# Last-hop finishes spread out and normed in place, remainder products and gates listed later, in a four-layer graph network on one core

## The chip, the cores and the metric

One NeuronCore of a Trainium2 chip runs the whole network as one launch. The metric is device time in microseconds, the median of several executions.

## The reference, cut to what matters

2708 nodes with 512 features, a dense fp32 matrix `adj` (2708 x 2708), four layers, each a residual with a layer norm:

```python
x = _layernorm(x + L0(x, adj))                # adj @ x with masked norms
x = _layernorm(x + L1(x, adj, adj, ...))      # gated: sigmoid(attn_a * x_a + attn_b * x_b)
x = _layernorm(x + L2(x, adj, weight))        # x@w0 + adj@x@w1 + adj^2@x@w2 + adj^3@x@w3: three hops
x = _layernorm(x + L3(x, adj, deg, W, b))     # relu((a_norm @ x + x) @ W + b)
```

## The kernel before

Each sweep over `adj` is cut into block products in a Strassen-like scheme, so that VectorE forms sums and differences of blocks (`z`, `s`, `t`) and TensorE multiplies them into four PSUM homes called u, c, d and a. The two sweep ranges of a hop have seven products each. Work is *listed*: `at(position, function)` puts a step at a position, one product being two units long, and a scheduler then orders each engine's instructions from that list. What happens is decided by the order that comes out, not by the listed number itself.

When an output block is complete, its *finish* runs in the product that follows: six tiles are transposed back (`ps_n`), added to their residual `ld`, normed, stored to `X3`, transposed again (`ps_t`) and stored to `X3T`. The last hop has four groups of such finishes.

```python
def nat(nm):                                    # six buffers of [128, 512] in all
    return pool.tile([P, D], F32, name=nm, tag="nat", bufs=6)

def fetch2(src, h, r0, w):                      # a tile of w rows, cut where it crosses a 128-row block
    o = nat("ld")
    for t, a, b, m in split(h, r0, w):          # m = 128, 82, 46, 36, 92, 83, 119, 74 or 9 rows
        nc.sync.dma_start(out=o[b : b + m, :], in_=src[t][a : a + m, :])
    return o

def done5(p0, dp, g, i0, n, h, cc, tiles):      # the finishes of the last hop
    for i, (s, lo, w) in enumerate(tiles):
        ...
        def a(...): got["x"] = fetch2(X2, h, r0, w)
        def b(...):
            ps = untranspose2(cc, s, lo, w)     # ps_n
            y = got["x"]
            nc.vector.tensor_tensor(y[:w], ps[:w], y[:w], ALU.add)
            o = nat("o")
            layernorm([(o, 0, D)], y, w, True)  # VectorE, GpSimd (power), VectorE, ScalarE
            store2(X3, o, h, r0, w)
            got["o"] = o
        def c(...): store_T(X3T[...], transposed([(got["o"], 0, D)], w)[:, :, :w])   # ps_t
        p = p0 + dp * i                         # dp = 0.15, for the last group 0.12
        at(p - 0.3, a); at(p, b); at(p + 0.5, c)
```

The loads of z for the next products stand in the same SyncE queue as these fetches:

```python
nc.sync.dma_start(out=t[:w, :n], in_=src)       # w = 128, or 74 for the remainder rows; a ring of 38 tiles
```

## Time and profile before

| | |
|---|---|
| time before | 3113.19 us (median of 3, 3111.91 to 3114.22) |
| span of the profiled execution | 3116.2 us |
| TensorE idle | 150 us of the span; the list of its waits adds up to 129 us, 22 of them in the counting at the start |
| waits in the finishes of the last hop | 46.0 us (ps_t, ps_n L1051) |
| waits of the second layer's gates (pz) | 16.9 us |
| waits of the remainder product (accu L987) | 15.2 us |

The number that matters is the idle time of TensorE with its aftermath (the slow clock after a wait: 0.80 to 0.87 granted in the four finish products of the last hop, 1.00 in a product without a wait), since it is busy for 95% of the span and every other engine has room (VectorE, the next, is busy for 70%). The prediction shows the lines.

### The profile page before, as it was taken

Reading aid. Unit: us, or ns where it says so; the run is one execution under the profiler, and the core shown is the slowest. Engines: PE = TensorE matmul, PEld = TensorE weight load, DVE = VectorE, ACT = ScalarE, POOL = GpSimd, SP = SyncE. Lnnn points to the kernel's source line nnn. Section 1 sums busy time; section 2 is a strip of 40 time slices with the busy share of each in tenths; the row PEclk is TensorE's granted clock in tenths of the full one; section 3 lists DMA queues with packets and bytes.
Section 4 is the critical chain, followed back from the end, with each engine's and each line's share of the span. In section 5 each row is a group of like instructions: output and inputs, shape, how many; then the busy total and the mean of one; then the engine's idle time right before and its main releaser. Section 6 shows DMA issues by size and latency. Waiting matters only on the chain.

```text
span 3116.2 us, 37246 instructions
## 1 busy us (share of the span) xinstructions
PE 2965.9 (95%) x10982; PEld 1943.1 (62%) x10982; DVE 2194.5 (70%) x5396; ACT 601.7 (19%) x1149; POOL 550.9 (18%) x985
## 2 busy tenths in 40 slices
PE   7999989999999999999999999999998898899995
PEld 5755655557665666766666666666665565565553
DVE  5889787565557676774776768767776576778684
ACT  4554100000154554531000000000001100101000
POOL 1423233232310101213101030011201202300000
PEclk9999999999999999999999999999999899999998
DMA  7665456556554334645766585566755556755551
GB/s 220 209 191 171 140 175 188 136 141 140 168 104 127 108 111 119 195 140 185 221 182 197 178 250 166 177 208 184 229 167 179 175 175 191 213 168 187 155 167 62
DMA packets 363251, 529.75 MB, mean 170 GB/s; under 512 B 49730, under 2 KB 309274, under 8 KB 363048
## 3 DMA queue, kind: packets, MB, share of 16 engines
q1 hardware_dynamic: 305020, 380.81, 42.9%
q0 software_dynamic: 48736, 135.73, 13.2%
q10 hardware_dynamic: 9292, 10.84, 1.1%
q8 instruction: 87, 1.43, 0.2%
q14 instruction: 116, 0.95, 0.1%
HBM read 436.81 MB, written 90.37 MB: 169 GB/s over the span
## 4 chain that ended last, share of the span: by engine, by line
PE 80%; DMA 9%; DVE 6%; issue 3%; POOL 1%; ACT 1%; SPq 0%; ACTq 0%; POOLq 0%; DVEq 0%
PE accd L982 11%; PE accc L982 10%; PE accu L982 10%; PE ps_d L470 8%; PE accu L342 8%; PE accd L342 7%; PE accc L342 7%; PE acca L982 5%; PE acca L342 4%; DMA ld<-X 2%; DMA z<-As 2%; DMA a<-in_adjT 1%; PE accu L987 1%; PE accd L987 1%; PE acca L987 1%
## 5 line engine op out<-in xcount | busy, mean ns | idle before, releaser
L942 DVE TENSOR_TENSOR z<-z 128x339 f32<-128x339 f32 (+1 forms) x966 | 463.6, 508 | 56.3 <-DMA z<-As 28.7
L982 PE MATMUL accc<-z,t 128*128 128x338 f32 (+1 forms) x644 | 216.3, 455 | 0.0
L424 POOL TENSOR_TENSOR rstd<-rstd,neg_half 128x1 f32<-128x1 f32 (+3 forms) x92 | 57.9, 630 | 848.9 <-DVE rstd L423 846.0
L982 PE MATMUL accu<-z,t 128*128 128x338 f32 (+1 forms) x644 | 199.6, 456 | 0.2 <-DVE z L942 0.2
L982 PE MATMUL accd<-z,t 128*128 128x338 f32 (+1 forms) x644 | 196.9, 448 | 0.1
L982 PE MATMUL accc<-s,t 128*128 128x338 f32 (+1 forms) x644 | 195.8, 448 | 0.8 <-DVE s L942 0.8
L306 DVE TENSOR_TENSOR a<-a,a 128x384 f32<-128x384 f32 (+4 forms) x363 | 178.6, 515 | 18.5 <-PE accu L342 15.9
L1008 ACT COPY q<-accu 128x338 f32<-128x338 f32 (+1 forms) x84 | 34.3, 443 | 783.4 <-PE accu L982 783.4
L942 DVE TENSOR_TENSOR s<-z 128x338 f32<-128x338 f32 (+1 forms) x322 | 153.6, 507 | 30.5 <-PE accc L982 15.5
L982 PEld LDWEIGHTS accc<-z,t 128*128 128x128 f32 x644 | 123.6, 193 | 62.9 <-issue 4.0
L1014 DVE TENSOR_TENSOR q<-q,accd 128x338 f32<-128x338 f32 (+1 forms) x112 | 56.4, 504 | 150.3 <-PE accd L982 149.9
L982 PEld LDWEIGHTS accu<-z,t 128*128 128x128 f32 x644 | 123.2, 194 | 60.2 <-issue 3.8
L982 PEld LDWEIGHTS accc<-s,t 128*128 128x128 f32 x644 | 120.4, 190 | 58.2 <-DVE s L942 1.6
L982 PEld LDWEIGHTS accd<-z,t 128*128 128x128 f32 x644 | 119.8, 190 | 56.9 <-issue 1.2
L732 DVE SCALAR_TENSOR_TENSOR deg<-a,deg 128x384 f32<-128x384 f32 (+5 forms) x168 | 82.4, 506 | 80.5 <-DMA a<-in_adjT 80.0
L797 ACT ACTIVATE e<-row,neg_s 128x384 f32<-128x384 f32 (+5 forms) x176 | 100.5, 571 | 82.1 <-DVE e L799 24.0
L799 DVE TENSOR_TENSOR e<-e,f 128x384 f32<-128x384 f32 (+5 forms) x176 | 87.6, 506 | 27.6 <-ACT f L798 26.3
L798 ACT ACTIVATE f<-row,neg_s 128x384 f32<-128x384 f32 (+5 forms) x176 | 99.9, 568 | 12.7 <-PE accc L342 6.2
L309 POOL DMA_DIRECT2D As<-a x132 | 70.9, 540 | 130.5 <-DVE a L306 83.5
L1064 ACT COPY y<-ps_n 128x512 f32<-128x512 f32 (+2 forms) x48 | 28.1, 585 | 326.4 <-issue 176.3
L553 DVE SCALAR_TENSOR_TENSOR s<-a,row 128x384 f32<-128x384 f32 (+5 forms) x168 | 83.4, 509 | 9.8 <-ACT row L541 8.2
L800 DVE SCALAR_TENSOR_TENSOR a<-a,e 128x384 f32<-128x384 f32 (+5 forms) x176 | 87.9, 507 | 2.3
(632 smaller groups left out, 6060.6 us busy)
## 6 DMA issues: line engine op xcount, KB each, us to landing
z<-As SPq DMA_DIRECT2D x320, 169.5 KB
z<-As SPq DMA_DIRECT2D x320, 169.0 KB
a<-in_adjT SPq DMA_DIRECT2D x240, 192.0 KB
z<-in_adjT SPq DMA_DIRECT2D x240, 169.5 KB
z<-in_adjT SPq DMA_DIRECT2D x240, 169.0 KB
a<-in_adjT SPq DMA_DIRECT2D x120, 165.0 KB
cl<-in_adjT POOLq DMA_DIRECT2D x80, 192.0 KB, 4.5
a<-in_adjT SPq DMA_DIRECT2D x113, 128.0 KB
```

The source lines that it names most:

```text
L306: nc.vector.tensor_tensor(A[r, dst, k][:w, :n], A[r, a, k][:w, :n], A[r, b, k][:w, :n], op)
L342: nc.tensor.matmul(B[home, c][:, :n], X[STAT[p], k][:w, c * P : (c + 1) * P], A[r, MOV[p], k][:w, :n], start=bool(start and k == k0), stop ...
L470: nc.tensor.matmul(o, lhs(c), r, start=c == 0 and n == 0, stop=c == DC - 1, skip_group_check=True)
L553: nc.vector.scalar_tensor_tensor(t[:w, :n], a[:w, :n], 0.0, row[R0, h][:w, :n], ALU.is_gt, ALU.mult)
L732: nc.vector.scalar_tensor_tensor(d[:w, :n], a[:w, :n], 0.0, d[:w, :n], ALU.not_equal, ALU.add)
L797: nc.scalar.activation(e[:w, :n], row[R0, h][0][:w, :n], AF.Exp, bias=neg_s[:w, t : t + 1])
L798: nc.scalar.activation(f[:w, :n], row[R0, h][1][:w, :n], AF.Exp, bias=neg_s01[:w, t : t + 1])
L799: nc.vector.tensor_tensor(e[:w, :n], e[:w, :n], f[:w, :n], ALU.min)
L800: nc.vector.scalar_tensor_tensor(a[:w, :n], a[:w, :n], 0.0, e[:w, :n], ALU.not_equal, ALU.mult)
L942: nc.vector.tensor_tensor(d[:, :n], Z[x + (k,)][:, :n], Z[y + (k,)][:, :n], op)
L982: nc.tensor.matmul(B[home][:, :n], stat(v, k), a[:, :n], start=bool(start and k == 0), stop=k == nk - 1, skip_group_check=True)
L987: nc.tensor.matmul(B[home][:, :n], groups[st, "R"][0][:w, c * P : (c + 1) * P], Z[p, 2, 0][:w, :n], start=False, stop=True, skip_group_che ...
```

## The change

Its intent is to give waits other work to hide behind. The edit has four parts: finishes of the first layer 0.2 unit later (but for one group), gates of the second layer 0.25 unit later, the remainder product into u with its combination later in every product of the hops and the last layer, and the finishes of the last hop normed in place and further apart.

```diff
@@ finishes of the first layer
-            p = p0 + dp * i
+            p = p0 + dp * i + (0.0 if last and not h else 0.2)
@@ gates of the second layer
-            at(p0 + dp * i, b)
+            at(p0 + 0.25 + dp * i, b)
@@ remainder products, their combinations and sums
-  for home, p, c, pos in (("c", 1, 0, 4.5), ("u", 1, 1, 4.7), ("d", 0, 1, 5.5), ("a", 0, 0, 6.5)):
+  for home, p, c, pos in (("c", 1, 0, 4.5), ("u", 1, 1, 6.1), ("d", 0, 1, 5.5), ("a", 0, 0, 6.5)):
   ... leave (1, 1, "u", 0): 4.9 -> 6.3, now behind (0, 1, "d", 0) at 6.02
   ... add (1, 1): 5.1 -> 6.4, (1, 0): 5.2 -> 5.1, (0, 1): 6.2 -> 6.1
@@ finishes of the last hop
-                o = nat("o")
-                layernorm([(o, 0, D)], y, w, True)
-                store2(X3, o, h, r0, w)
-                got["o"] = o
+                layernorm([(y, 0, D)], y, w, True)
+                store2(X3, y, h, r0, w)
 ...
-            p = p0 + dp * i
-            at(p - 0.3, a)
+            p = p0 + 0.1 + 0.24 * i
+            at(p - 0.5, a)
             at(p, b)
-            at(p + 0.5, c)
+            at(p + 0.85, c)
```

More of the change, by code (lines that the diff above doesn't have):

```diff
@@ L1016, in sweep2 @@
                 for p, c, home, first, pos in ((0, 0, "u", 1, 1.02), (1, 1, "c", 1, 2.02), (1, 1, "d", 0, 3.02),
-                                               (1, 0, "u", 1, 4.02), (0, 1, "u", 1, 4.03), (1, 1, "u", 0, 4.9),
-                                               (1, 0, "c", 0, 5.02), (0, 1, "d", 0, 6.02), (0, 0, "a", 0, 7.02)):
+                                               (1, 0, "u", 1, 4.02), (0, 1, "u", 1, 4.03),                                                (1, 0, "c", 0, 5.02), (0, 1, "d", 0, 6.02), (1, 1, "u", 0, 6.3),
+                                               (0, 0, "a", 0, 7.02)):
                     at(b + u * pos, lambda a=(p, c, home, first), f=leave: f(*a))
@@ L1027, in add @@
                     nc.vector.tensor_tensor(Q[x, p, c][:, :n], Q[x, p, c][:, :n], Q[y, p, c][:, :n], ALU.add)
-                for p, c, pos in ((1, 1, 5.1), (1, 0, 5.2), (0, 1, 6.2), (0, 0, 7.1)):
+                for p, c, pos in ((1, 0, 5.1), (0, 1, 6.1), (1, 1, 6.4), (0, 0, 7.1)):
                     for i, (x, y) in enumerate(after):
@@ L1082, in b @@
                 nc.vector.tensor_tensor(y[:w], ps[:w], y[:w], ALU.add)
-                o = nat("o")
-                layernorm([(o, 0, D)], y, w, True)
-                store2(X3, o, h, r0, w)
-                got["o"] = o
+                layernorm([(y, 0, D)], y, w, True)
+                store2(X3, y, h, r0, w)
             def c(s=s, lo=lo, w=w, got=got):
-                store_T(X3T[g, h, s][:, lo : lo + w], transposed([(got["o"], 0, D)], w)[:, :, :w])
-            p = p0 + dp * i
-            at(p - 0.3, a)
+                store_T(X3T[g, h, s][:, lo : lo + w], transposed([(got["x"], 0, D)], w)[:, :, :w])
+            p = p0 + 0.1 + 0.24 * i
+            at(p - 0.5, a)
             at(p, b)
-            at(p + 0.5, c)
+            at(p + 0.85, c)
     for s, hop, src, done in ((3, 2, Y0, hop_done(Y1)), (4, 1, Y1, hop_done(Y2)), (5, 0, Y2, done5)):
```

## The prediction

The engines that it finds 0.58 busy are the 16 DMA engines, in the window from 2353.77 to 2400.73 us.

> **What bounds the kernel now.** I read the page's busy line first, then the chain of waits that ended last, then the list of what TensorE waited for, and only then single products, cut out as windows.
>
> ```profile
> PE 2965.9 (95%) x10982; PEld 1943.1 (62%) x10982; DVE 2194.5 (70%) x5396; ACT 601.7 (19%) x1149; POOL 550.9 (18%) x985
> PE 80%; DMA 9%; DVE 6%; issue 3%; POOL 1%; ACT 1%; SPq 0%; ACTq 0%; POOLq 0%; DVEq 0%
> ...
> PE ps_t L459 <- ACT o L429: 33.6, 11, 5.6
> ...
> PE pz L759 <- DVE P1c L383: 16.9, 6, 5.2
> PE accu L987 <- DVE q L1014: 15.2, 3, 8.8
> PE ps_n L1051 <- DVE ld L1082: 12.4, 2, 8.1
> PE ps_n L453 <- DVE P1c L383: 9.2, 2, 8.6
> ```
>
> TensorE is busy for 95% of the span of 3116.2 us; the next engine, VectorE, for 70%. The change takes no matmul away, so all it can win is TensorE's idle time and what hangs on it. In the list (total us, times, longest) ps_t and ps_n L1051 belong to the finishes of the last hop, 33.6 + 12.4 = 46.0 us; pz to the gates of the second layer; accu to the remainder product into home u in the second sweep; ps_n L453 to the finishes of the first layer. The counting at the start (19.1 us, left out above) is not touched.
>
> An idle gap costs more than its length. In one finish of the last hop (start, duration, group, idle before):
>
> ```profile
> 2605.79 1.12 PE L1051 MATMUL ps_n<-ident,q 128*83 128x128 f32 x4 [8.07 <-DVE ld L1082]
> ...
> 2623.43 0.82 PE L459 MATMUL ps_t<-ident,o 83*128 83x83 f32 x4 [3.03 <-ACT o L429]
> 2624.04 3.31 PE L982 MATMUL accd<-z,B22C 128*128 128x339 f32 x6
> ...
> 2629.47 1.87 PE L982 MATMUL acca<-z,B22C 128*128 128x339 f32 x6
> ```
>
> The same six matmuls take 3.31 us just after a wait and 1.87 us six microseconds later. So the product that holds the gap is what must be measured. The columns of the windows are: window and its length, busy of PE, PEld, DVE, ACT and POOL, granted clock, DMA share, GB/s.
>
> ```profile
> 2327.61:2353.77 26.16, 26.16 (x93) 17.46 (x92) 18.09 (x40) 1.67 (x4) 0.00 (x0) 1.00 0.57 168
> 2353.77:2400.73 46.96, 36.23 (x142) 24.14 (x141) 28.32 (x74) 9.42 (x16) 13.16 (x21) 0.85 0.58 182
> 2426.88:2479.28 52.40, 37.96 (x141) 24.69 (x140) 27.17 (x68) 9.12 (x16) 15.84 (x26) 0.80 0.55 176
> 2584.22:2633.46 49.24, 36.15 (x141) 24.32 (x140) 30.84 (x75) 7.76 (x12) 18.63 (x32) 0.86 0.63 191
> 2659.70:2700.09 40.39, 31.98 (x127) 21.34 (x126) 24.18 (x65) 9.43 (x16) 22.38 (x38) 0.87 0.77 233
> 2700.09:2722.27 22.18, 22.18 (x79) 14.80 (x78) 20.90 (x45) 1.67 (x4) 0.00 (x0) 1.00 0.61 183
> 1839.48:1868.28 28.80, 28.80 (x118) 19.82 (x117) 14.42 (x31) 5.12 (x10) 13.59 (x26) 1.00 0.86 277
> ```
>
> Row one is a product of the last hop without a finish, the next four are the products that carry the four groups of three finish tiles, row six is a short product without a finish, and row seven a product of an earlier hop with its finish, which runs at clock 1.00 without a wait. A finish of the last hop has 48 small transposes, 12 groups of four at 0.44 us of TensorE pitch, 5.3 us. Bare finish products would thus be 26.16 + 5.3 = 31.5 us, and the short one 22.18 + 5.3 = 27.5 us. The excess is 15.5 + 20.9 + 17.7 + 12.9 = 67.0 us: 46 of waits, some 20 of slow clock.
>
> Why the waits arise shows in the first finish:
>
> ```profile
> 2362.90 0.30 SPq L888 DMA_DIRECT2D ld<-X  x1
> ...
> 2374.05 0.69 DVE L1082 TENSOR_TENSOR ld<-ps_n,ld 128x512 f32<-128x512 f32 x1 [6.37 <-DMA ld<-X]
> 2374.66 0.15 DVE L423 TENSOR_SCALAR rstd<-mv 128x1 f32<-128x1 f32 x1
> 2375.91 0.81 ACT L429 ACTIVATE o<-ld,rstd 128x512 f32<-128x512 f32 x1 [3.37 <-DVE rstd L426]
> 2376.78 1.12 PE L459 MATMUL ps_t<-ident,o 128*128 128x128 f32 x4 [5.42 <-ACT o L429]
> ```
>
> The fetch of a later tile's residual is issued at 2362.90 and releases VectorE only at 2374.05, 11 us on. VectorE stands at the sum of that tile (L1082) for 6.37 us; the variance step (L423) of the tile before stands behind it, and so do ScalarE's norm and TensorE's transposes. The fetch is late because six buffers serve twelve tiles (a fetched one and a normed one, o, for each of the six finish halves): SyncE's queue waits three times for o, 8.0 us in all, and its fetches take turns with the loads of z.
>
> [...] 3.31 against 1.87 us, and granted clocks of 0.80 to 0.87 in just these windows. [...] L423 had its data and started only after L1082's 6.37 us. [...] the trace has the 11 us landing in a window where those engines are 0.58 busy. An earlier issue is therefore worth its lead, not a shorter transfer.
>
> **The change part by part.**
>
> Last hop. The norm is written in place, so the o tile goes: a group needs 6 buffers instead of 12, which is all there are, and no fetch of a group waits for its own norms. Fetches are listed 0.5 of a unit ahead of their sums instead of 0.3; in the emitted order they stand 30 to 40 rows earlier on SyncE in groups one to three, a few rows earlier in group four. The transposes are listed 0.85 after instead of 0.5. In the new order 36 matmuls of 0.284 us and three groups of 0.44 us lie between a tile's arrival in PSUM and its transposes, 10.2 + 1.3 = 11.5 us, against some 5.9 before. What must fit in there, from the trace: VectorE 0.69 (sum) + 0.69 + 0.18 (statistics) + 0.14, GpSimd 0.57, VectorE 0.16, ScalarE 0.81, which is 3.24 us, and 4 to 5 with the hand-offs. So it fits, as long as VectorE's queue ahead is under 6 us. VectorE is the tight one: 28.3, 27.2, 30.8 and 24.2 us of work in products that become 31.5 (27.5) long. I leave 2 us of excess for each group, 8 in all: 67 − 8 = 59 us gained.
>
> Gates of the second layer. Listed 0.25 of a unit later, pz stands 12 matmuls further back in TensorE's order: 3.87, 2.6 and 3.3 us in the three ranges that wait. The waits there are 3.5, 4.3 + 3.2 and 5.2 us; with slow clock the excess over the usual pitch is 7.7, 11.0 and 9.2, together 27.9 us. The first goes (7 us). The second and third go in part, as VectorE itself waits 7.79 us for in_adjT, until 707.42, just ahead of the second: 2.5 to 3.5 and 3.3 to 7 us. Sum 13 to 17, taken as 14.
>
> Remainder product into u. It moves behind the products into c and d and the first part of a, and its combination (leave) behind that of d, so TensorE has other work while VectorE forms the remainder's. Its waits:
>
> ```profile
> 2917.75 1.50 PE L987 MATMUL accu<-z,T2R 74*128 74x339 f32 x2 [6.20 <-DVE q L1014]
> ...
> 3061.57 0.93 PE L987 MATMUL accu<-z,B21R 74*128 74x339 f32 x1 [8.76 <-DVE q L1014]
> ```
>
> With the clock that is 9.4 and about 11 us. But VectorE was late in both places because it stood 7.79 us for z (until 2915.93) and 10.60 us for x3T (until 3055.41), and the product into d needs combinations queued behind the same waits. I count 5 and 4: 9 us.
>
> First layer. Only groups that show no wait are moved by 0.2; the last group, whose ps_n waits 8.57 us, keeps its place by the exception in the edit. 0 us.
>
> Given back: the bank of u is held longer, later transposes push the stores of X3T towards the next load of it, and everything after moves to other DMA traffic. I put 4 us on it. Sum: 59 + 14 + 9 − 4 = 78; the rows of small spread rounded down, 73 to 78 us. From 3113.2 that is 3035 to 3040, and I take 3040 us, 2.3% less.
>
> **The rivals.** First, VectorE takes over in the last hop: its 30.8 us in the third finish product leave 0.7 us of slack in 31.5. If its queue runs behind, ps_t waits stay, named after ScalarE as now, at perhaps 4 to 5 us of excess a group more: 3040 becomes about 3058. Against it speaks that much of VectorE's work there is for combinations which TensorE needs only in the next product. Second, buffers of the transposed tile: a store of X3T takes 5.9 to 6.8 us to land in this trace, there are two buffers, and tiles now come every 0.24 unit, some 3.8 us at full pace, so two spacings are 7.6 us. That is just enough; on GpSimd[...], the power for the next tile's norm may stand behind loads waiting for such a store, in the last group above all. Two waits of 3 us with their slow clock would be some 10 us: 3050. Third, the remainder's and gates' waits only move, because DMA and not the listing is late: 9 + 7 us fall away, 3056. Fourth, the fetches stand so early that they displace z loads and the product itself waits for z; SyncE's waits for free z buffers speak against it, since it already runs ahead of TensorE by whole buffers.
>
> **Range and chances.** All of it working without a residue is 67 + 17 + 9 = 93 us, 3020. Two of the rivals together give 3066 to 3074. I put 8 in 10 between 3022 and 3070. Faster by over 2% needs 62.3 us (under 3050.9): the last hop alone gives nearly that by my sum, and any two rivals forfeit it. Chances: 0.70 faster by over 2%, 0.29 within 2%, 0.01 slower by over 2%; for the last I see no mechanism.
>
> **What would show each step.** Right: ps_t waits fall from 33.6 us to under 6 and ps_n L1051 from 12.4 to under 3; the four finish products read 31 to 34 us (short one 27 to 30) at clocks over 0.95; SyncE waits no more for o in the last hop; pz falls from 16.9 to under 8, accu L987 from 15.2 to under 8; ps_n L453 stays near 9. TensorE's busy time should fall too, by about 25 us, from matmuls no longer run at a low clock. Wrong: a DVE or ACT wait of over 4 us left in a finish product (first rival), GpSimd or ps_t waiting on a store of X3T (second), new waits for z in products that had none, or accd waiting in place of accu. The prediction fails as a whole if the last-hop windows stay above 38 us: then listing order was not what held them.

## More of the kernel before

The features stored in `X3` are read back at once, into the tiles B22, B21, B11 and T3 of the last layer (issued from GpSimd), and VectorE forms the sums T1, T2 and T4 from them.

## The result, and the profile after

The changed kernel took 3074.14 us (median of 4, 3066.36 to 3081.57) against 3113.7 us before (4 runs): a ratio of 0.987, 95% interval 0.9844 to 0.9897. Ratios here are the mean of one kernel's runs over the mean of the other's of the same rounds, so they are not quite the ratio of the medians. That is some 40 us faster; 73 to 78 had been predicted, and 3074 lies outside the range of 3022 to 3070. The execution that was profiled is the fastest of the four, 3064.6 us of span, so the trace shows a gain of 51.6 us.

The busy line and the chain of waits of the changed kernel:

```profile
PE 2953.7 (96%) x10982; PEld 1934.7 (63%) x10982; DVE 2189.4 (71%) x5396; ACT 596.6 (19%) x1145; POOL 552.5 (18%) x985
PE 74%; DMA 9%; DVE 8%; issue 6%; POOL 2%; ACT 1%; SPq 0%; POOLq 0%; ACTq 0%; DVEq 0%
```

What its TensorE waited for (total us, times, longest):

```profile
PE accd L982 <- DVE z L942: 12.5, 5, 5.9
PE ps_n L453 <- DVE P1c L383: 10.2, 2, 9.8
PE accc L987 <- DMA z<-in_adjT: 6.6, 2, 4.2
PE pz L759 <- DVE P1c L383: 6.6, 2, 3.6
```

The waits that the edit aimed at are gone or smaller: no ps_t wait for o is left in the list (0.8 us for ld is, 0.6 before, outside the last hop), accu L987 neither, and pz fell from 16.9 to 8.9 us (the 6.6 shown and a new 2.3 for C L383). New ones stand in their place: accd waits for combinations, and accc for a load of z itself (L987 is the remainder product, L982 the full ones). The busy time fell by 12 us, not by the 25 that were expected, so new slow-clock stretches have come up too (0.89 to 0.95 granted in four of the products below).

The windows show where. These are products of the last hop in the changed kernel. The first is the one in which the fetches of group one are issued, four products ahead of that group's finish; from the finish on, products without a loss are left out. The columns are the window and its length, the busy times of PE, PEld, DVE, ACT and POOL, the granted clock, the DMA share and GB/s:

```profile
2237.72:2272.51 34.79, 30.20 (x93) 19.04 (x92) 24.73 (x52) 1.67 (x4) 0.00 (x0) 0.90 0.58 173
2350.99:2381.68 30.69, 30.65 (x134) 21.20 (x132) 27.23 (x72) 8.50 (x14) 12.22 (x19) 1.00 0.69 214
2381.68:2415.36 33.68, 29.53 (x102) 19.34 (x101) 19.22 (x44) 1.02 (x2) 1.52 (x2) 0.90 0.61 189
2415.36:2447.81 32.45, 30.72 (x133) 21.13 (x132) 28.63 (x74) 8.46 (x14) 14.87 (x24) 1.00 0.75 229
2553.82:2584.34 30.52, 30.52 (x134) 21.29 (x133) 27.32 (x69) 6.84 (x10) 15.97 (x25) 1.00 0.76 236
2584.34:2616.55 32.21, 28.71 (x101) 18.84 (x100) 19.12 (x43) 1.02 (x2) 10.00 (x19) 0.95 0.80 234
2616.55:2643.52 26.97, 26.68 (x120) 18.55 (x118) 21.39 (x59) 6.78 (x12) 14.49 (x26) 1.00 0.84 263
2643.52:2675.41 31.89, 25.93 (x87) 16.46 (x86) 25.27 (x57) 3.77 (x8) 7.96 (x13) 0.89 0.63 185
```

Rows two, four, five and seven are the finish products: 30.69, 32.45, 30.52 and 26.97 us, at clock 1.00. Before they took 46.96, 52.40, 49.24 and 40.39 us. That is 68.4 us won, more than the 59 predicted, though some 3 us of it are transposes that moved into the next product (134 matmuls instead of 142 here, 102 instead of 93 there). The other rows are products that had taken 26.2 us (the last one 22.2) before and had no wait at all. The first is now 34.79, the one behind group one 33.68, behind three 32.21, behind four 31.89 us. (The one behind group two, not shown, is 27.31 us, of which some 0.9 us are transposes that now fall into it.) Together they grew by 159.9 − 127.0 = 32.9 us. So half of what the finishes won is given back in other products of the hop.

Two mechanisms can be read off. Ahead of group one, SyncE's queue (start, duration, group):

```profile
2234.50 3.14 SPq L930 DMA_DIRECT2D z<-in_adjT  x1
2237.69 0.62 SPq L930 DMA_DIRECT2D z<-X2T  x1
2238.49 6.71 SPq L888 DMA_DIRECT2D ld<-X  x4
```

And the window within that time, with columns as above:

```profile
2240.00:2246.00 6.00, 6.00 (x23) 4.02 (x22) 2.97 (x7) 0.88 (x2) 0.00 (x0) 1.00 0.16 54
```

The fetches of group one are issued here, some 115 us before their finish at 2353.83 us. Before, all but two of them were issued from 2354 on. Four fetches take 6.71 us to issue (0.42 to 2.62 us each), and one load of z ahead of them took 3.14, where 0.3 to 0.4 us is usual. The window of the same time shows the DMA engines busy for 0.16 only, at 54 GB/s: SyncE is jammed while the DMA engines idle. Loads of z that stand behind are what TensorE waits for at 2260.51 us (2.41 us, for in_adjT).

Behind groups three and four, VectorE and TensorE:

```profile
2599.67 0.96 DVE L268 TENSOR_TENSOR T4A<-B21A,T2A 128x768 f32<-128x768 f32 x1 [8.94 <-DMA B21A<-X]
...
2602.44 4.00 PE L982 MATMUL accc<-z,t 128*128 128x339 f32 x8 [3.50 <-DVE q L1014]
...
2659.47 0.69 DVE L265 TENSOR_TENSOR T1D<-T3D,B11D 128x512 f32<-128x512 f32 x1 [4.40 <-DMA B11D<-X]
...
2665.64 3.75 PE L982 MATMUL accd<-z,B21C 128*128 128x338 f32 x6 [5.94 <-DVE z L942]
```

VectorE stands at a sum for the last layer, whose tile is still being reloaded from the features just stored; combinations that TensorE needs now are queued behind it.

### The profile page after: what moved, and what is told of

Same layout as the page of the kernel before. It is cut to its first block, busy times and chain, and to the rows that moved or that the text cites. A ratio compares the mean times of both kernels' runs of the same rounds, so it can differ in the third digit from the quotient of the medians.

```text
span 3064.6 us, 37270 instructions
## 1 busy us (share of the span) xinstructions
PE 2953.7 (96%) x10982; PEld 1934.7 (63%) x10982; DVE 2189.4 (71%) x5396; ACT 596.6 (19%) x1145; POOL 552.5 (18%) x985
## 4 chain that ended last, share of the span: by engine, by line
PE 74%; DMA 9%; DVE 8%; issue 6%; POOL 2%; ACT 1%; SPq 0%; POOLq 0%; ACTq 0%; DVEq 0%
PE accc L982 10%; PE accd L982 9%; PE accu L982 9%; PE accu L342 8%; PE ps_d L470 8%; PE accc L342 8%; PE accd L342 7%; PE acca L982 4%; PE acca L342 3%; DMA z<-in_adjT 1%; DMA ld<-X 1%; DVE z L942 1%; PE ps_n L1051 1%; DVE t L963 1%; PE accc L987 1%
## 5 line engine op out<-in xcount | busy, mean ns | idle before, releaser
L982 PE MATMUL accc<-z,t 128*128 128x338 f32 (+1 forms) x644 | 206.9, 454 | 3.5 <-DVE q L1014 3.5
L982 PE MATMUL accu<-z,t 128*128 128x338 f32 (+1 forms) x644 | 197.0, 451 | 2.0 <-DVE z L942 2.0
L982 PE MATMUL accc<-s,t 128*128 128x338 f32 (+1 forms) x644 | 196.5, 449 | 1.3 <-DVE s L942 1.3
L982 PE MATMUL accd<-z,t 128*128 128x338 f32 (+1 forms) x644 | 196.0, 448 | 0.4 <-DVE z L942 0.4
L982 PEld LDWEIGHTS accc<-z,t 128*128 128x128 f32 x644 | 123.2, 193 | 67.1 <-issue 4.9
L982 PEld LDWEIGHTS accu<-z,t 128*128 128x128 f32 x644 | 121.7, 192 | 62.7 <-issue 4.5
L982 PEld LDWEIGHTS accd<-z,t 128*128 128x128 f32 x644 | 120.5, 190 | 59.5 <-DVE z L942 2.3
L982 PEld LDWEIGHTS accc<-s,t 128*128 128x128 f32 x644 | 120.2, 190 | 59.7 <-DVE s L942 3.3
L470 PE MATMUL ps_d<-w,q 128*128 128x512 f32 (+2 forms) x192 | 89.3, 612 | 5.7 <-DVE q L1119 5.7
```

The source lines that it names most:

```text
L470: nc.tensor.matmul(o, lhs(c), r, start=c == 0 and n == 0, stop=c == DC - 1, skip_group_check=True)
L982: nc.tensor.matmul(B[home][:, :n], stat(v, k), a[:, :n], start=bool(start and k == 0), stop=k == nk - 1, skip_group_check=True)
```

## The experiments

Fifteen kernels ran, in four sets. The kernels of one set shared one chip and the runs of before on it; ratios compare with those. Between sets only ratios are compared.

### Set one: each part alone

Each kernel is the one before with only one part of the diff shown above: the finishes of the last hop (`hop_only`), the gates (`gates_only`), the remainder (`rest_only`), the first layer (`first_only`).

> Only the finishes of the last hop are changed (norm in place, 0.24 spacing, transposes 0.85 later); everything else as before. The prediction on record (A) gave this part 59 us. Rival B, read from the trace of the changed kernel: the four finish products do lose their whole excess of 67 us, but about 30 us come back as new waits (8.6 us while TensorE waits for z around the first group's fetches, 5.3 us likewise around the second's, 7.1 and 9.0 us where the sums for the last layer wait for their reload). A expects 59 us less than before, B 30 to 40 us less, with the same waits for z<-in_adjT in the product before the first group of finishes.

> Only the gates of the second layer are listed 0.25 unit later. Predicted 14 us; the two traces differ by 12.1 us across that layer. If that part stands by itself: 11 to 14 us less than before. If the gain there was due to an earlier part of the change: under 6 us.

> Only the remainder product into u, its combination and the sums behind it are listed later. Predicted 9 us; the traces show 4.7 us across the last layer, with a wait of 5.3 us at accd where accu waited 8.8 us. If the wait only moves to accd: 4 to 6 us less than before. If the last hop's new waits (accd 5.94 us) come from this part rather than from the finishes, this kernel shows them too and gains nothing or loses.

> Only the finishes of the first layer, all but the last group, are listed 0.2 unit later. Predicted 0 us. The traces differ by some 4 us the wrong way across that layer (ps_n waits 9.8 us against 8.6, running sums 1.4 us more). If that is the edit: 2 to 4 us slower than before. If it is scatter between executions: within 1 us of before.

| kernel | median us | ratio to before (95%) | difference |
|---|---|---|---|
| before | 3118.44 | | |
| hop_only | 3081.94 | 0.9889 (0.9869 to 0.9909) | −35 us |
| gates_only | 3109.19 | 0.9963 (0.9943 to 0.9984) | −12 us |
| rest_only | 3116.17 | 0.9990 (0.9972 to 1.0008) | −3 us |
| first_only | 3121.94 | 1.0013 (0.9995 to 1.0030) | +4 us |

(Differences: ratio less one, times 3118.) They add up to −46 us, against −40 for the whole change; each has an interval of some ±6 us, so the parts are independent as far as can be seen. The last hop gives 35 us, as B had it and not A. Its trace has the same losses in the same places: 33.98 us for the product ahead of group one, 34.03, 34.16 and 30.79 us behind groups one, three and four. So these losses belong to the finishes, not to the moved remainder. In the trace of rest_only accu no longer waits, and accd waits 8.2 us instead: the wait moved on to the next product that needs the same late combinations.

A warning lies in this set too. The pz waits, in code that hop_only, rest_only and first_only do not touch, were 20.4, 27.3 and 21.4 us in the three traces, and 16.9 in that of before. They scatter by 10 us from one execution to the next. The prediction had taken one trace's 16.9 us as the amount. And the trace of gates_only itself shows 16.7 us (12.4, and 4.3 in a new wait for C L383), no less than before: the 12 us rest on the times of its six executions, and its own trace does not show where they were won.

### Set two: what holds the z loads back

Theory E of the expectations is an estimate from the changed kernel's trace: the transfers from 2240 to 2246 us move at 54 GB/s and a share of 0.16 of the 16 DMA engines (0.13 until 2244, the work of 2.1 engines), so few engines would carry the fetches issued there, and z loads would wait for them.

> The changed kernel, but each fetch of a residual piece in the last hop (82, 46, 36, 92, 83, 119, 74 or 9 rows) is issued as two transfers: the largest multiple of 16 rows, and the rest of under 16 rows. Same bytes, same place in SyncE's queue. Theory E (few engines): [...] then the 8 and 5.5 us lost around the fetches of groups one and two go, 10 to 14 us less than the changed kernel, about 52 us less than before, and DMA issue times of over 1 us disappear. Theory Q (queue order): the fetches cost because they and their waits for a buffer stand in front of z in SyncE's queue; then within 3 us of the changed kernel.

```diff
 def fetch2(src, h, r0, w):
     for t, a, b, m in split(h, r0, w):
-        nc.sync.dma_start(out=o[b : b + m, :], in_=src[t][a : a + m, :])
+        m0 = m // 16 * 16 if src is X2 else 0
+        for e, f in ((0, m0), (m0, m)):
+            if f > e:
+                nc.sync.dma_start(out=o[b + e : b + f, :], in_=src[t][a + e : a + f, :])
```

> The changed kernel, but the residuals of the last hop are fetched from ScalarE's queue instead of SyncE's. Theory Q (queue order): z loads are no longer held back, 10 to 14 us less than the changed kernel, unless ScalarE's own copies stand behind a fetch that waits. Theory E (few engines): [...] 0 to 6 us less than the changed kernel.

```diff
-        nc.sync.dma_start(out=o[b : b + m, :], in_=src[t][a : a + m, :])
+        eng = nc.scalar if src is X2 else nc.sync
+        eng.dma_start(out=o[b : b + m, :], in_=src[t][a : a + m, :])
```

> The kernel before with only the fetches of the last hop split as in after_split16; buffers, places and spacing as before. If the late landing of the fetches (7.6 to 11 us) was a matter of few DMA engines: landings of 3 to 5 us, the two waits of ps_n for ld (12.4 us) go and the finish products lose 15 to 30 us of their excess of 67. If it was the buffers alone: under 8 us gained.

The edit is that of after_split16, in the kernel before.

> The kernel before with the norm in place only: no o tile, but the old spacing (0.15 and 0.12) and the transposes 0.5 after, fetches listed 0.3 ahead. If the buffers were the whole cause of the last hop's waits: as good as hop_only or better (35 us or more less than before), since it finishes earlier and so reloads earlier. If the distance of the transposes matters as well: ps_t waits of 10 to 25 us stay and it gains 10 to 25 us.

```diff
-                o = nat("o")
-                layernorm([(o, 0, D)], y, w, True)      # in place as in the change
+                layernorm([(y, 0, D)], y, w, True)
                 ...
             p = p0 + dp * i                              # spacing and places as before
```

| kernel | median us | ratio to before (95%) |
|---|---|---|
| before | 3116.02 | |
| after_split16 | 3046.41 (3046.21 to 3047.17) | 0.9777 (0.9762 to 0.9793) |
| after_actq | 3080.73 | 0.9889 (0.9869 to 0.9909) |
| before_split16 | 3084.97 | 0.9892 (0.9874 to 0.9911) |
| inplace_only | 3093.60 | 0.9924 (0.9909 to 0.9940) |

Splitting the fetches, with the same bytes at the same place in the same queue, brings the changed kernel to 0.9777, some 70 us under before, where 52 were expected. The products in which the fetches of groups one and two were issued, ahead of group one's finish and behind it, have no wait again:

```profile
2238.22:2264.37 26.15, 26.15 (x93) 17.45 (x92) 24.88 (x53) 1.67 (x4) 0.00 (x0) 1.00 0.72 217
2373.44:2400.37 26.93, 26.93 (x102) 18.12 (x101) 23.64 (x53) 1.02 (x2) 1.52 (x2) 1.00 0.77 231
```

(26.15 us instead of 34.79, 26.93 instead of 33.68, of which 0.8 us are transposes: 15.4 of the 20 us between the two traces.) The scatter between executions shrank from 15 us to 1 us as well. Moving the fetches to another queue did not help: at 0.9889 the kernel is no faster than the changed kernel's 0.987. Its trace shows one reason. What SyncE waited for between 2230 and 2262 us, where the fetches of group one are issued (total us, times, longest):

```profile
SPq L931 <- DMA ld<-X: 14.7, 5, 4.4
```

No fetch stands in SyncE's queue any more, and each z load takes the usual 0.3 to 0.4 us to issue. Yet by the profile SyncE waits 14.7 us for fetches to land, against 6.3 us in the changed kernel (why a z load waits for them is not shown). So z is held back even where no fetch stands before it in its queue, which speaks against theory Q. The time alone would not be a clean test, since ScalarE's own copies now stand behind the fetches: TensorE waits 3.31 us for one at 2243.67.

What a split changes shows in the DMA share. Where the changed kernel has 54 GB/s at a share of 0.16, the trace of after_split16 has 163 GB/s at 0.64 from 2236 to 2242 us, while SyncE issues eight of the split fetches, and 229 GB/s at 0.78 from 2242 to 2248. That fits few engines before the split and more after it, but which engines they are, no run here shows, and no run counts them.

Even the kernel before gains 1.08% by the split alone. Its finish products:

```profile
2356.88:2393.34 36.46, 32.30 (x141) 21.43 (x140) 26.62 (x70) 9.41 (x16) 13.10 (x21) 1.00 0.71 224
2419.50:2456.73 37.23, 33.20 (x141) 22.66 (x140) 23.46 (x62) 9.20 (x16) 16.17 (x26) 0.95 0.73 228
2561.67:2603.63 41.96, 35.28 (x141) 23.50 (x140) 30.32 (x74) 7.76 (x12) 18.89 (x32) 0.92 0.76 225
2629.87:2667.58 37.71, 31.42 (x128) 21.50 (x126) 24.01 (x63) 9.43 (x16) 22.11 (x38) 0.86 0.81 237
```

Together they take 153.4 us instead of 189.0: of the excess of 67 us that the prediction put down to buffers and listing, 36 went with nothing but a different row count per transfer (15 to 30 were expected). Waits of ps_t fell from 33.6 to 20.0 us, those of ps_n for ld from 12.4 to 0.7. inplace_only shows the share of the buffers: −0.76%, 24 us, with 6.8 us of ps_t waits left of 33.6. It pays a loss ahead of group one as hop_only does (36.18 us there, hop_only 33.98), with the fetches listed where they were: it is the freed buffers that let them go early. Its gain is within the 10 to 25 us expected if the distance mattered, but the ps_t waits fell below the 10 us that went with it: the buffers took away most of those waits, and waits of ps_n (7.8 us) and accu (5.4 us) stand beside the rest.

### Set three: a control, and the rest of the losses

> A control to after_split16: the changed kernel with each odd piece fetched as two halves (82 rows as 41 and 41, 46 as 23 and 23, 36 as 18 and 18, and so on), so as many transfers as in after_split16, but with row counts that 16 does not divide. Theory E[...]: no gain, within 1% of the changed kernel or slower than it, and the stretch of low DMA rate ahead of the first finish stays. If smaller or more transfers were what helped: as good as after_split16, about 2.2% less than before.

```diff
-        m0 = m // 16 * 16 if src is X2 else 0
+        m0 = m // 2 if src is X2 and m % 16 else 0     # 82 = 41 + 41: as many transfers, 16 divides none
```

> after_split16 with the finishes of groups three and four closer (0.17 apart instead of 0.24, transposes 0.7 after instead of 0.85). Theory R (reload): the 5.5 and 6.9 us still lost in the products behind those groups are the sums for the last layer, which wait for results that are stored and reloaded; with the spread the last store comes later. Then these two shrink to 0 to 6 us together: 5 to 12 us less than after_split16, unless ps_t waits come back. If the loss is instead GpSimd's queue or VectorE's order whatever the spacing: within 3 us of after_split16.

```diff
-            p = p0 + 0.1 + 0.24 * i
+            p = p0 + 0.1 + (0.17 if g else 0.24) * i
-            at(p + 0.85, c)
+            at(p + (0.7 if g else 0.85), c)
```

> after_split16, with the fetches of the last layer and all 74-row loads of z split likewise into 64 and 10 rows. If the few-engine transfers cost elsewhere too: 3 to 15 us less than after_split16. If the z loads have slack enough and the extra issues on SyncE cost as much: within 3 us.

```diff
-                    nc.sync.dma_start(out=t[:w, :n], in_=src)          # loads of z
+                    w0 = w // 16 * 16
+                    nc.sync.dma_start(out=t[:w0, :n], in_=src[:w0])
+                    if w > w0:
+                        nc.sync.dma_start(out=t[w0:w, :n], in_=src[w0:w])
```

> after_split16 without the first part of the change (finishes of the first layer at their old places). first_only was 0.13% slower than before with an interval that includes nothing; if the edit really costs, this is 3 to 5 us less than after_split16, whose scatter is under 1 us; if that was scatter, within 1 us.

The edit: after_split16 with `p = p0 + dp * i` in the first layer, as before.

| kernel | median us | ratio to before (95%) |
|---|---|---|
| before | 3116.31 | |
| after_halves | 3114.21 | 0.9999 (0.9982 to 1.0016) |
| split_tight | 3050.67 | 0.9785 (0.9772 to 0.9798) |
| split_z | 3033.50 | 0.9736 (0.9724 to 0.9749) |
| split_nofirst | 3040.36 | 0.9757 (0.9745 to 0.9770) |

after_halves shows that it is the row count, and not the number or size of the transfers. The same number of small transfers as after_split16, but with 41 rows, takes the whole gain of the change away. Its windows, the product ahead of group one and six microseconds within it:

```profile
2243.33:2293.84 50.51, 30.13 (x94) 18.99 (x92) 26.24 (x55) 1.67 (x4) 0.00 (x0) 0.80 0.39 119
2246.00:2252.00 6.00, 6.00 (x23) 4.02 (x22) 2.68 (x7) 0.88 (x2) 0.00 (x0) 1.00 0.07 25
```

Its SyncE queue just then:

```profile
2243.16 18.82 SPq L891 DMA_DIRECT2D ld<-X  x8
```

The rate is 25 GB/s at a share of 0.07 of the 16 engines, about what one of them would be (0.0625). The product takes 50.51 us, 24.4 more than the bare one, where the changed kernel lost 8.6. The sizes fit: group one has three pieces of 82 and three of 46 rows, 384 rows of 2048 bytes, 786 kB. At 54 GB/s that is 14.6 us, at 25 GB/s 31.5, a difference of 16.9 us; the product grew by 50.51 − 34.79 = 15.7. That engines are what a row count costs is an estimate from these two shares and rates.

split_z goes on with the same cure: the 74-row loads of z and the fetches of the last layer are split too, for another 0.4% (against after_split16, in another set), 13 us, near the top of its expected 3 to 15. split_tight did not help: at 0.9785 it is as fast as after_split16, and in its trace VectorE waits 10.12 us for B21A and 9.50 us for B11D. The two products behind these groups still lose 11.6 us together (10.8 in after_split16, transposes left out), where 0 to 6 were expected, and 3.6 us of ps_t waits came back. So the wider spacing is not what makes the reload late; theory R in that form fell. split_nofirst stands 0.2% below after_split16 (in another set). Together with first_only this suggests that the first part of the change costs some 4 to 6 us, though neither shows it alone beyond doubt. (The expectation says that first_only's interval "includes nothing"; it is 0.9995 to 1.0030 and does include no change.)

### Set four: the reload, and the sum with clean fetches

> after_split16 with the sums for the last layer built from the features before the hops instead of from this hop's results (a wrong result on purpose): the same loads from GpSimd's queue into the same tiles, but none has to wait until a finish has stored. Theory R (store and reload): both losses behind groups three and four go, the waits of accc and accd there (2.1 and 4.5 us) are gone and it takes 10 to 14 us less than after_split16. If the first of them is a matter of the tile that TensorE still holds, or of the order of VectorE's queue: the wait of T4A for B21A stays and only the second goes, 5 to 8 us less.

```diff
-    next_x2(S[6], X3)
+    next_x2(S[6], X2)      # wrong result on purpose: does not wait for this hop's stores
```

> The kernel before with all the split transfers of split_z and nothing of the change. before_split16 took 1.08% less than before; the 74-row loads of z should add some 0.4% as they did in split_z. If the change as a whole is worth more once the fetches are spread over the engines (62 to 80 us by the sum of its parts without the new waits): this kernel stands 40 to 55 us above split_z. If split transfers alone do the work and the change adds what it showed by itself: about 40 us or less above split_z.

The edit: the kernel before with the splits of fetches and z loads.

> The parts that helped, together: the change without its first part, all fetches and z loads split into multiples of 16 rows and a rest. split_z was 2.64% less than before, leaving the first part out was worth about 0.2%: 2.8% less than before, some 3028 us.

The edit: before_split_z with the gates, the remainder and the last hop changed, the first layer not.

| kernel | median us | ratio to before (95%) |
|---|---|---|
| before | 3125.23 | |
| reload_other (wrong result) | 3045.58 | 0.9743 (0.9720 to 0.9767) |
| before_split_z | 3066.05 | 0.9800 (0.9778 to 0.9822) |
| best | 3035.27 | 0.9713 (0.9691 to 0.9735) |

The products behind groups three and four in reload_other:

```profile
2577.55:2607.56 30.01, 27.54 (x101) 17.97 (x100) 23.47 (x52) 1.02 (x2) 9.98 (x18) 1.00 0.85 251
2634.03:2656.97 22.94, 22.94 (x87) 15.38 (x86) 18.99 (x48) 3.90 (x8) 5.02 (x8) 1.00 0.73 221
```

Behind group four the loss is gone (22.94 us, 29.87 in after_split16): it was the wait for this hop's results to be stored and read back, which in the kernel before probably passed unseen within the 13 us of excess of the finish itself. Behind group three it stays (30.01 us, 31.09 in after_split16), with VectorE still at B22C for 4.99 us and at B21A for 1.55. There the reload does not wait for the stores; whether the tile is held by TensorE too long or the sum stands too early in VectorE's order is left open, for a loss of some 3 us. That is the second of the two outcomes expected; the ratio, 11 us under after_split16 in another set and with a scatter of 22 us, cannot tell the two apart.

best is as fast as split_z within the intervals; the two are the fastest kernels, 2.6 to 2.9% under before. In the kernel before, splitting the z loads and the fetches of the last layer too brought 0.9% on top of before_split16 (in another set), twice the 0.4% expected. And before_split_z answers the last question: with the transfers split the change, without its first part, is worth 31 us by the medians (3066.05 − 3035.27) and 27 by the ratios, within some 10: less than the 40 us, or some 44 without the first part, that it took off the kernel before. The two cures overlap: the split fetches alone had already taken 36 of the 67 us of excess in the finish products.

## Why the prediction was wrong, point by point

- **Last hop, the finish products: right in kind, too small.** Clock 1.00 and no ps_t wait, as foreseen; 68.4 us won instead of 59, some 3 of them moved transposes.
- **"Given back: ... I put 4 us on it": this is the term that failed.** It measured 32.9 us in the profiled execution. The fourth rival named one of its two mechanisms, fetches that displace z loads, and was dismissed "since it already runs ahead of TensorE by whole buffers". It is what happened ahead of and behind group one (8.6 and 6.8 us of transfer jam, by comparison with after_split16). Behind groups three and four, 6.0 + 9.7 us less 1.8 us of transposes, some 14 us, come with VectorE's waits for tiles of the last layer that are being reloaded, which was not among the rivals at all. Behind group four it is shown to be the store and reload of this hop's results; behind group three the cause of part of it stays open.
- **"An earlier issue is therefore worth its lead, not a shorter transfer": wrong.** The 11 us landing was taken as given, with a DMA share of 0.58 as its cause; that cause was an estimate. The landing was slow because of the row counts; before_split16 and after_halves show it, −1.08% for a split into multiples of 16, with ps_n's waits for ld down from 12.4 to 0.7 us, and the whole gain lost for halves. That such row counts are carried by few engines is an estimate from the measured shares, 0.16 with pieces of 82 and 46 rows and 0.07 with halves of them.
- **"30 to 40 rows earlier": not taken for the time it stands for.** In the trace the fetches of group one moved from 2354 to 2225–2245 us, four products and more ahead, into a stretch that had two fetches before and now has nine.
- **Gates: right in size.** 14 predicted, 12 measured, with an interval of 5 to 18 us (the ratio's interval times 3118). The sign given, pz under 8 us, just failed (8.9), and the trace of gates_only does not show the gain in its waits.
- **Remainder: right direction, a third of the size.** 9 predicted, 3 measured with an interval that includes 0; the wait moved to accd, as the prediction's third rival had it.
- **First layer: 0 predicted, some 4 us lost**, the interval of first_only just including 0.

The sum as it came out: 68 + 12 + 3 − 4 − 33 = 46 us, between the 40 us of the times and the 52 us of the trace. The prediction's 3066 to 3074 for "two of the rivals together" meets the measured 3074, but by luck: the first two rivals did not come true (the finish products show no ps_t wait), the third came true for the remainder alone, and the fourth was not in that sum.

## What to carry to other kernels

Before moving transfers about, look at the row count of each. Here SyncE took 1.7 us (6.71 us for 4) and 2.4 us (18.82 us for 8) to issue one at DMA shares of 0.16 and 0.07, and splitting such transfers into a multiple of 16 rows and a short rest was worth 1.1% by itself and 2% with all loads, against 1.3% for the whole reordering. A freed buffer is also a freed transfer: ask when it will now be issued and which loads will stand behind it. And a stage that loses its waits can uncover the next dependency, here the reload of what it had just stored, so the products around it must be in the sum.
